# RWKV time mixing of a Perceiver block: token shift folded into the weights, keys kept in PSUM, gate moved into the denominator

## The chip, the cores and the metric

The kernel runs on one core of a Trainium2 chip, in float32. The metric is the device time of one execution in microseconds (us); lower is better. TensorE (PE) multiplies matrices into PSUM, VectorE (DVE), ScalarE (ACT) and GpSimd (POOL) work on tiles of 128 partitions, and loads and stores are issued from queues: SyncE (SP) carries most of them, ACT and POOL some.

## The reference

The program is a network of four layers; each has cross attention to a context, self attention or a relative of it, and a feed-forward part. X holds 8 sequences of 64 steps with 256 channels (512 tokens). The change lies in the second stage of layer 1, which mixes along time as RWKV does. For each sequence, with `xx` the input one step earlier (zero at the first):

```python
xk = x * time_mix_k + xx * (1.0 - time_mix_k)      # xv, xr alike
k = xk @ Wk.T; v = xv @ Wv.T; sr = sigmoid(xr @ Wr.T)
w = -exp(time_decay); u = time_first
def step(carry, kv):                                # along time, per channel
    aa, bb, pp = carry
    kt, vt = kv
    ww = u + kt
    p = max(pp, ww)
    e1 = exp(pp - p); e2 = exp(ww - p)
    y = (e1 * aa + e2 * vt) / (e1 * bb + e2)
    ww2 = pp + w
    p2 = max(ww2, kt)
    e1b = exp(ww2 - p2); e2b = exp(kt - p2)
    return (e1b * aa + e2b * vt, e1b * bb + e2b, p2), y
out = (sr * y) @ Wo.T
```

It is applied to a normalised X, and the result is added to X. `pp` keeps the exponents small: the sums aa and bb are stored relative to exp(pp).

## The kernel before

X stays in SBUF as 4 tiles (NI = 4) of 128 tokens by 256 channels. A stage normalises X (`normed`: statistics on DVE at L343 and L345, a power of -1/2 on POOL at L347, the scaling on DVE at L351), turns it with PE transposes (`transposed`, L378: tiles called pst) into `T`, two chunks (NC_ = 2) of 128 channels by 512 tokens, and multiplies it by weights: `lin_T` (L396, psl) gives a transposed result, `lin_nat` (L405, psn) a result in X's own layout. `into_X` (L1254) adds a PSUM tile into X. `evac` (L334 on ACT, L336 on DVE, in turns) copies a PSUM tile to SBUF.

The stages that matter, in order:

- f0, a mixture of experts. Its end: the experts' results are scattered to DRAM by indirect DMAs on POOL (L1234, 15 times in the last round), and `collect` loads them back in home order as `got` (L1249, tiles 0 and 2 from SP's queue, 1 and 3 from ACT's) and adds them to X (L1251). The experts' weights lie in a pool, `weights0`, that is closed after it.
- x1, the cross attention of layer 1: norm, projections (ends at L1622), then `flash` over the four tiles of tokens, which loads the context as `cn` and `ct` (L1630, L1632), takes maxima (L658), and exponentials (L671); its output goes into X at L1254.
- r1, the time mixing, L1671 to L1739. For k, v and r in turn DVE builds the mixed input: T times the share (L1689), plus T one step earlier times one minus the share (L1690; 504 of the 512 columns, since 8 first steps have no predecessor). PE multiplies by the weights, in 4 matmuls for each of the three. Keys kk and values vv are evacuated to SBUF, and r goes through Sigmoid on ACT (L1695). The recurrence runs along the 512 columns as DVE scans: pp (L1715) with a decay row whose value at each sequence's first step is -3e38, which resets it; then bb (L1728) and aa (L1729). The exponents e1, e2, f1, f2 each come from a difference on DVE and an Exp on ACT (L1716 to L1725). Then den = f1*bb + f2, the numerator f1*aa + f2*vv, a reciprocal (L1735), two products (L1736 and L1738, the second by the gate rr). All of that is done for each half c of the 256 channels.
- f1, another mixture of experts; it begins with X's norm and its transposes.

Weights are loaded by `weight(name)` (L307 to L313, the DMA at L312) into a rotating pool of six slots of 1 MB: x1q, x1kv, r1a (Wk and Wv), r1b (Wr and Wo), f1g, then the pairs f1up and f1dn of f1's experts. A slot's load waits until the last reader of what lay there is done. In f1, DVE, PE and the loads go on in step for eight experts.

A tile framework takes the instructions, gives each engine its own queue, and sets semaphores from the tiles that are read and written. The queue of an engine is in the order in which the framework schedules, by priority and readiness, not strictly in the order of the text[...]. Tiles with the same tag share space; pools that are closed give their space to later ones.

Of the kernel before, what the change touches and what calls it, by code (L numbers as in the profile page):

```python
# [11 lines left out]
F32 = mybir.dt.float32  # L12
AF = mybir.ActivationFunctionType
ALU = mybir.AluOpType
# [258 lines left out]
def perceiver(ctx: ExitStack, tc: tile.TileContext, d, col_at, row_at, const_at, out):  # L273
# [27 lines left out]
    def col(name, c=0):  # L301
        n, _ = col_at[name]
        return cols[:, n + c : n + c + 1]
# [3 lines left out]
    def weight(name, e=None):  # L307
        src = d[name] if e is None else d[name][e]
        n = src.shape[1]
        assert n <= WSLOT, (name, n)  # L310
        t = wpool.tile([P, WSLOT], F32, tag="w", name=f"w_{name}_{e}")
        nc.sync.dma_start(t[:, :n], src)  # L312
        return t[:, :n]  # L313

    def chunks(w, n):
        return w.rearrange("p (k n) -> p k n", n=n)
# [14 lines left out]
    def evac(dst, src):  # L331
        turn[0] ^= 1
        if turn[0]:
            nc.scalar.copy(dst, src)  # L334
        else:
            nc.vector.tensor_copy(dst, src)  # L336
# [916 lines left out]
    def into_X(i, t):  # L1253
        nc.vector.tensor_tensor(X[:, i, :], t, X[:, i, :], ALU.add)  # L1254
# [12 lines left out]
    def general(n=8):  # L1267
        return tc.tile_pool(name="ps", bufs=n, space=PSUM)
# [31 lines left out]
    with tc.tile_pool(name="l0res", bufs=1) as res, ExitStack() as both:  # L1300
# [38 lines left out]
        def fetch(b):  # L1339
            if b < B:  # L1340
                cns[b] = load_nat(cpool, b, 3)
# [261 lines left out]

    with tc.tile_pool(name="x1", bufs=1) as pool:
        wq = chunks(weight("x1q"), C)
        wkv = weight("x1kv")
# [15 lines left out]
        with ps as ps, psS as psS, psO as psO, fp as fp:  # L1624
# [36 lines left out]
                return dict(scores=scores, av=av, done=done, shift=qb[:, i : i + 1], before={1: [lambda: fetch(i + 1)] if i + 1 < NI else []})  # L1661

            fetch(0)
            flash(ps, psS, psO, fp, [tile_of(i) for i in range(NI)])
        with general() as ps:
            add_row_to_X("x1bv")
# [1 line left out]

    with general() as ps, tc.tile_pool(name="r1", bufs=1) as pool:  # L1671
        NC_ = C // P
        wkv, wro = chunks(weight("r1a"), C), chunks(weight("r1b"), C)
        xT = transposed(ps, normed(X))
        b4 = lambda x: x.rearrange("p c (b s) -> p c b s", s=S)
        g3 = lambda x: x.rearrange("p c (b s) -> p (c b) s", s=S)

        def big(name, n=NT):
            return pool.tile([P, NC_, n], F32, tag=name, name=name)

        om = pool.tile([P, 6], F32, tag="om", name="om")
        for n, k in enumerate("kvr"):
            for c in range(NC_):
                nc.vector.tensor_scalar(om[:, 2 * n + c : 2 * n + c + 1], col("time_mix_" + k, c), -1.0, 1.0, ALU.mult, ALU.add)
        kk, vv, rr = big("kk"), big("vv"), big("rr")
        for n, (k, w, dst) in enumerate((("k", wkv[:, 0:2], kk), ("v", wkv[:, 2:4], vv), ("r", wro[:, 0:2], rr))):
            mixed = pool.tile([P, NC_, NT], F32, tag="mixed", name="mixed", bufs=2)
            for c in range(NC_):
                nc.vector.tensor_scalar(mixed[:, c, :], xT[:, c, :], col("time_mix_" + k, c), None, ALU.mult)  # L1689
                nc.vector.scalar_tensor_tensor(  # L1690
                    b4(mixed)[:, c, :, 1:], b4(xT)[:, c, :, : S - 1], om[:, 2 * n + c : 2 * n + c + 1],
                    b4(mixed)[:, c, :, 1:], ALU.mult, ALU.add,
                )
            if k == "r":
                lin_T(ps, w, mixed, C, lambda c, t: nc.scalar.activation(rr[:, c, :], t, AF.Sigmoid))  # L1695
            else:
                lin_T(ps, w, mixed, C, lambda c, t: evac(dst[:, c, :], t))

        wd = pool.tile([P, NC_], F32, tag="wd", name="wd")
        n0, _ = col_at["time_decay"]
        nc.scalar.activation(wd, cols[:, n0 : n0 + NC_], AF.Exp)
        nc.vector.tensor_scalar(wd, wd, -1.0, None, ALU.mult)
        decay, pp, e1, e2, ev = big("decay"), big("pp"), big("e1"), big("e2"), big("ev")
        aa, bb, yy = big("aa"), big("bb"), big("yy")
        for c in range(NC_):
            nc.scalar.activation(decay[:, c, :], ones[:, 0:1].to_broadcast([P, NT]), AF.Copy, scale=wd[:, c : c + 1])
        nc.gpsimd.memset(g3(decay)[:, :, 0:1], -3.0e38)
        nc.gpsimd.memset(g3(e1)[:, :, 0:1], 0.0)  # L1710
        at = lambda x, c: b4(x)[:, c]
        old, new = (lambda x, c: at(x, c)[:, :, : S - 1]), (lambda x, c: at(x, c)[:, :, 1:])
        pmax, f1, f2, den = big("pmax"), big("f1"), big("f2"), big("den")
        for c in range(NC_):
            nc.vector.tensor_tensor_scan(pp[:, c, :], decay[:, c, :], kk[:, c, :], 0.0, ALU.add, ALU.max)  # L1715
            nc.vector.scalar_tensor_tensor(new(e1, c), old(pp, c), wd[:, c : c + 1], new(pp, c), ALU.add, ALU.subtract)  # L1716
            nc.scalar.activation(new(e1, c), new(e1, c), AF.Exp)
            nc.vector.tensor_tensor(e2[:, c, :], kk[:, c, :], pp[:, c, :], ALU.subtract)
            nc.scalar.activation(e2[:, c, :], e2[:, c, :], AF.Exp)
            u = col("time_first", c)  # L1720
            nc.vector.scalar_tensor_tensor(new(pmax, c), new(kk, c), u, old(pp, c), ALU.add, ALU.max)
            nc.vector.tensor_tensor(new(f1, c), old(pp, c), new(pmax, c), ALU.subtract)
            nc.scalar.activation(new(f1, c), new(f1, c), AF.Exp)
            nc.vector.scalar_tensor_tensor(new(f2, c), new(kk, c), u, new(pmax, c), ALU.add, ALU.subtract)
            nc.scalar.activation(new(f2, c), new(f2, c), AF.Exp)  # L1725
        for c in range(NC_):
            nc.vector.tensor_tensor(ev[:, c, :], e2[:, c, :], vv[:, c, :], ALU.mult)
            nc.vector.tensor_tensor_scan(bb[:, c, :], e1[:, c, :], e2[:, c, :], 0.0, ALU.mult, ALU.add)  # L1728
            nc.vector.tensor_tensor_scan(aa[:, c, :], e1[:, c, :], ev[:, c, :], 0.0, ALU.mult, ALU.add)  # L1729
            nc.vector.tensor_tensor(new(den, c), old(bb, c), new(f1, c), ALU.mult)  # L1730
            nc.vector.tensor_tensor(new(den, c), new(den, c), new(f2, c), ALU.add)
            nc.vector.tensor_tensor(new(f2, c), new(f2, c), new(vv, c), ALU.mult)
            nc.vector.tensor_tensor(new(f1, c), new(f1, c), old(aa, c), ALU.mult)
            nc.vector.tensor_tensor(new(f1, c), new(f1, c), new(f2, c), ALU.add)
            nc.vector.reciprocal(new(den, c), new(den, c))  # L1735
            nc.vector.tensor_tensor(new(f1, c), new(f1, c), new(den, c), ALU.mult)  # L1736
            nc.scalar.copy(at(f1, c)[:, :, 0:1], at(vv, c)[:, :, 0:1])
            nc.vector.tensor_tensor(yy[:, c, :], f1[:, c, :], rr[:, c, :], ALU.mult)  # L1738
        lin_nat(ps, wro[:, 2:4], yy, into_X)  # L1739

# [251 lines left out]
```

## Time and profile before

| | us |
|---|---|
| median of 3 runs | 2175.82 (2172.9 to 2176.54) |
| the profiled execution | 2174.78 |
| its span on the core | 2173.0 |
| mean granted clock of TensorE | 0.949 |
| first pst of x1's norm | 825.16 |
| first score matmul of x1 | 839.19 |
| first matmul of r1's projections | 895.95 |
| last product of r1 (yy) ends | 933.37 |
| last pst of f1's norm starts | 941.48 |

The last five rows are starts or ends in the span of the profiled execution. In the lines of the profile, "L396" is a line of the kernel, `out<-in` the tiles, and square brackets show for how long the engine was idle just before and who released it. A semaphore wait is put down to the one that came last. POOL's queue and SP's queue are as much queues as PE's.

### The profile page before, as it was taken

What the parts mean: (1) busy time and instruction counts of PE and PEld (TensorE: products, weight loads), DVE (VectorE), ACT (ScalarE), POOL (GpSimd) and SP (SyncE); (2) the same over time, 40 slices, a digit from 0 to 9 for tenths busy, and PEclk for the clock granted to TensorE, in tenths of its full rate; (3) what the DMA queues carried; (4) which work ended last, traced back from release to release, by engine and by line L of the source; (5) the groups of instructions that cost most, each with busy time, mean ns of one, the idle gap of its engine ahead of it and who ended that gap; (6) DMA issues with size and microseconds to landing.
All of it is one profiled execution on the core that took longest, in us unless ns stands there. A gap on an engine that the chain in (4) does not pass through costs nothing. (4 is left out here: it accounts for less than half of the span.)

```text
span 2173.0 us, 35537 instructions
## 1 busy us (share of the span) xinstructions
PE 1959.8 (90%) x14824; PEld 1398.1 (64%) x14824; DVE 1269.5 (58%) x2132; ACT 1025.3 (47%) x1672; POOL 310.8 (14%) x381
## 2 busy tenths in 40 slices
PE   5879999999987997569999999999899899998889
PEld 5546777777756574348567777778755566665747
DVE  6456777776627223750266666664623588888733
ACT  2326667666412222202255555552211788887323
POOL 3311111110033120030000000001000122222214
PEclk9989999999988998869999999999899999999979
DMA  6310000000014206116300001100111000000312
GB/s 232 116 47 1 17 17 16 17 17 11 11 61 170 95 34 260 70 42 236 129 16 32 32 32 42 37 1 30 59 49 60 30 33 17 17 18 16 132 61 100
DMA packets 33695, 130.97 MB, mean 60 GB/s; under 512 B 4408, under 2 KB 14272, under 8 KB 29056
## 3 DMA queue, kind: packets, MB, share of 16 engines
q1 hardware_dynamic: 29856, 120.57, 15.6%
q0 software_dynamic: 2592, 7.09, 0.9%
q8 instruction: 117, 1.92, 0.4%
q10 hardware_dynamic: 1088, 1.05, 0.1%
q14 instruction: 42, 0.34, 0.0%
HBM read 121.08 MB, written 13.66 MB: 62 GB/s over the span
## 5 line engine op out<-in xcount | busy, mean ns | idle before, releaser
L867 PEld LDWEIGHTS psav<-cn,raw 128*128 128x128 f32 (+1 forms) x3328 | 403.0, 192 | 88.5 <-issue 87.2
L802 DVE TENSOR_TENSOR raw<-raw,mb 128x1024 f32<-128x1024 f32 (+1 forms) x336 | 383.9, 1146 | 60.3 <-ACT mb L798 60.3
L867 PE MATMUL psav<-cn,raw 128*128 128x129 f32 (+1 forms) x3328 | 406.9, 275 | 0.7 <-ACT raw L806 0.7
L855 PE MATMUL psS<-qk,ct 128*128 128x512 f32 (+1 forms) x832 | 397.7, 600 | 6.8 <-ACT raw L856 6.8
L780 DVE TENSOR_TENSOR top<-raw,top 128x1024 f32<-128x1024 f32 (+1 forms) x240 | 271.4, 1131 | 152.6 <-ACT raw L856 123.4
L806 ACT ACTIVATE raw<-raw 128x1024 f32<-128x1024 f32 (+1 forms) x336 | 335.4, 1001 | 15.7 <-DVE raw L802 14.2
L856 ACT COPY raw<-psS 128x512 f32<-128x512 f32 (+1 forms) x416 | 236.3, 586 | 126.6 <-PE psS L855 123.4
L855 PEld LDWEIGHTS psS<-qk,ct 128*128 128x128 f32 (+1 forms) x832 | 140.7, 187 | 129.2 <-issue 95.5
L347 POOL TENSOR_TENSOR mv<-mv,mhalf 128x1 f32<-128x1 f32 x76 | 41.8, 553 | 872.1 <-DVE mv L346 861.4
L977 ACT COPY raw<-psS 128x1024 f32<-128x1024 f32 (+1 forms) x112 | 105.3, 940 | 2.2 <-PE psS L972 1.9
L774 DVE TENSOR_TENSOR top<-raw 128x1024 f32<-128x1024 f32 x48 | 58.8, 1226 | 70.9 <-ACT raw L856 36.8
L972 PEld LDWEIGHTS psS<-qz,kT 32*128 32x128 f32 (+1 forms) x1664 | 54.8, 181 | 61.5 <-ACT raw L977 33.7
L972 PE MATMUL psS<-qz,kT 32*128 32x128 f32 (+1 forms) x1664 | 77.0, 296 | 15.0 <-ACT raw L977 14.8
L993 PE MATMUL psav<-raw,v 128*32 128x128 f32 (+1 forms) x1664 | 87.2, 282 | 3.6 <-ACT raw L806 3.5
L993 PE MATMUL psav<-raw,ones 128*32 128x128 f32 (+1 forms) x1664 | 84.6, 275 | 0.0
L798 ACT COPY mb<-psmb 128x512 f32<-128x512 f32 x48 | 28.1, 585 | 96.9 <-PE psmb L796 96.8
L1208 PE MATMUL psgd<-w,xdT 128*128 x212 | 63.6, 436 | 0.8 <-DVE xdT L1197 0.4
L796 PE MATMUL psmb<-dg,ones 128*128 128x512 f32 x96 | 53.6, 640 | 7.9 <-POOL dg L790 4.6
L950 PE MATMUL psk<-ct,w_x3kv_None 128*128 128x401 f32 (+1 forms) x128 | 58.0, 539 | 0.7 <-ACT qT L334 0.7
L960 PE MATMUL psv<-w_x3kv_None,ct 128*128 128x256 f32 (+1 forms) x208 | 55.6, 388 | 0.0
L788 DVE TENSOR_REDUCE nm<-psm 128x4 f32<-128x512 f32 x48 | 33.0, 687 | 37.1 <-PE psm L786 36.8
L993 PEld LDWEIGHTS psav<-raw,v 128*32 128x32 f32 (+1 forms) x1664 | 41.1, 110 | 20.0 <-ACT raw L806 5.7
(438 smaller groups left out, 2948.4 us busy)
## 6 DMA issues: line engine op xcount, KB each, us to landing
cn<-in_cn_dram SPq DMA_DIRECT2D x24, 838.5 KB, 4.5
ct<-in_ct_dram SPq DMA_DIRECT2D x24, 800.5 KB, 4.5
w<-in_f0w_dram SPq DMA_DIRECT2D x8, 1088.0 KB, 15.5
w_f1up<-in_f1up_dram SPq DMA_DIRECT2D x8, 1024.0 KB, 4.9
w_f1dn<-in_f1dn_dram SPq DMA_DIRECT2D x8, 1024.0 KB, 4.8
w_f2w<-in_f2w_dram SPq DMA_DIRECT2D x8, 768.0 KB, 4.2
w<-in_f3w_dram SPq DMA_DIRECT2D x16, 384.0 KB, 7.6
dealt<-in_deal_dram SPq DMA_DIRECT2D x2, 2955.5 KB, 21.8
```

The costliest lines, as they stand in the source:

```text
L774: nc.vector.tensor_tensor(hd["top"], hd["raw", 0], raw, ALU.max)
L780: nc.vector.tensor_tensor(top[:n, :m, :], raw, top[:n, :m, :], ALU.max)
L802: nc.vector.tensor_tensor(raw, raw, halves[h]["mb"][:n].unsqueeze(1).to_broadcast([n, m, 512]), ALU.add)
L806: nc.scalar.activation(raw, raw, AF.Exp)
L855: nc.tensor.matmul(x[:n], ct[:, kt * P : kt * P + n], qk, start=True, stop=True)
L856: nc.scalar.copy(raw[:n, i, :], x[:n])
L867: nc.tensor.matmul(oa[:, j // 2, j % 2 * CO : (j % 2 + 1) * CO], w[:n, i, j * P : (j + 1) * P], cn[:n, kt, :], start=kt == 0 and j % 2 == ...
L950: nc.tensor.matmul(t[:, : hi - lo], wkv[:, c * P : (c + 1) * P], cts[b][:, lo:hi], start=True, stop=True)
L972: nc.tensor.matmul(x[:n, g, i * P : (i + 1) * P], kTs[h][r, kt * P : kt * P + n], qzs[b][r, c].rearrange("p m s -> p (m s)"), start=True, ...
L977: nc.scalar.copy(raw[:n, :m, :].rearrange("p i (g s) -> p i g s", g=4), x[:n, :, : m * P].rearrange("p g (i s) -> p i g s", s=P))
L993: nc.tensor.matmul(oa[r, at * P : (at + 1) * P], what, w[:n, i, g * P : (g + 1) * P], start=kt == 0 and at == 0, stop=kt == KT - 1 and at ...
L1208: nc.tensor.matmul(y[:, :m], st[t]["xT"][:, k, :], w[:, bass.ds(x + at + k * m, m)], start=k == 0, stop=k == C // P - 1)
```

## The change

Five things change in r1, and one new function is called within x1.

- The shares are multiplied into the weights instead of into the input: `mix_weights()` makes six pairs of 128x256 tiles, weight times share and weight times one minus share, on POOL, and it is called in x1 just before `flash`. It also makes wd (minus the exponential of the decay) and loads Wo into a tile of its own, `wo`. Its tiles are in the pool `mixw`, opened after `weights0` is closed.
- `mix(n)` then adds four matmuls on T and four on T one step earlier (504 columns) into one PSUM tile of two banks; there are three such tiles, for k, v and r. Keys are read from PSUM by the scan and by the differences. Values are copied by ACT.
- e1 and e2 come from one difference de: e1 = exp(-Relu(de)), e2 = exp(-Relu(-de)). f1 and f2 come from df in the same way. So there is no pmax, and there are two activations (Relu, Exp) for each.
- The gate: instead of y times sigmoid(r), den is multiplied by 1 + exp(-r) (`er`, with exp on ACT and a min and add on POOL), ahead of the reciprocal.
- ev, f2*vv and den*er are done on POOL.
- The output's eight matmuls write one PSUM tile, `mixed_out`, and the four additions follow.

In the order of the queues, POOL's om and first two products come ahead of the last scatter of f0, and the rest ahead of x1's four norm powers; SP's w_f1dn comes ahead of `got`; the loads of f1's weights move forward, since r1a and r1b are free earlier; ACT loads the table of exp ahead of `got`'s issue. The scheduler's order on ACT in r1 is e1, e2, f1, f2 of half 0, then e1 of half 1, the copies of vv, the rest of half 1, and er last.

```diff
--- before.py
+++ after.py
@@ -1603,6 +1603,28 @@
+    NC_ = C // P
+    mixing = ExitStack()
+    mixp = mixing.enter_context(tc.tile_pool(name="mixw", bufs=1))
+    mixw = mixp.tile([P, 3, 2, NC_, C], F32, tag="mixw", name="mixw")
+    wd = mixp.tile([P, NC_], F32, tag="wd", name="wd")
+    om = mixp.tile([P, 3, NC_], F32, tag="om", name="om")
+    wo = mixp.tile([P, NC_, C], F32, tag="wo", name="wo")
+    def mix_weights():
+        n0, _ = col_at["time_decay"]
+        nc.scalar.activation(wd, cols[:, n0 : n0 + NC_], AF.Exp)
+        nc.gpsimd.tensor_scalar(wd, wd, -1.0, None, ALU.mult)
+        nc.sync.dma_start(wo.rearrange("p k n -> p (k n)"), d["r1b"][:, 2 * C :])
+        r1a, r1b = chunks(weight("r1a"), C), chunks(weight("r1b"), C)
+        for n, (k, w) in enumerate((("k", r1a[:, 0:2]), ("v", r1a[:, 2:4]), ("r", r1b[:, 0:2]))):
+            for c in range(NC_):
+                share = col("time_mix_" + k, c)
+                nc.gpsimd.tensor_scalar(om[:, n, c : c + 1], share, -1.0, 1.0, ALU.mult, ALU.add)
+                nc.gpsimd.tensor_scalar(mixw[:, n, 0, c, :], w[:, c, :], share, None, ALU.mult)
+                nc.gpsimd.tensor_scalar(mixw[:, n, 1, c, :], w[:, c, :], om[:, n, c : c + 1], None, ALU.mult)
     with tc.tile_pool(name="x1", bufs=1) as pool:
         wq = chunks(weight("x1q"), C)
         wkv = weight("x1kv")
@@ -1661,6 +1683,7 @@
                 return dict(scores=scores, av=av, done=done, shift=qb[:, i : i + 1], before={1: [lambda: fetch(i + 1)] if i + 1 < NI else []})
             fetch(0)
+            mix_weights()
             flash(ps, psS, psO, fp, [tile_of(i) for i in range(NI)])
         with general() as ps:
             add_row_to_X("x1bv")
@@ -1668,75 +1691,84 @@
-    with general() as ps, tc.tile_pool(name="r1", bufs=1) as pool:
-        NC_ = C // P
-        wkv, wro = chunks(weight("r1a"), C), chunks(weight("r1b"), C)
+    with general(2) as ps, tc.tile_pool(name="r1", bufs=1) as pool, tc.tile_pool(name="r1p", bufs=1, space=PSUM) as held:
         xT = transposed(ps, normed(X))
         b4 = lambda x: x.rearrange("p c (b s) -> p c b s", s=S)
         g3 = lambda x: x.rearrange("p c (b s) -> p (c b) s", s=S)
-        def big(name, n=NT):
-            return pool.tile([P, NC_, n], F32, tag=name, name=name)
-        om = pool.tile([P, 6], F32, tag="om", name="om")
-        for n, k in enumerate("kvr"):
+        at = lambda x, c: b4(x)[:, c]
+        old, new = (lambda x, c: at(x, c)[:, :, : S - 1]), (lambda x, c: at(x, c)[:, :, 1:])
+        def big(name):
+            return pool.tile([P, NC_, NT], F32, tag=name, name=name)
+        def mix(n):
+            kvr = held.tile([P, NC_, NT], F32, tag=f"mix{n}", name="mix")
             for c in range(NC_):
-                nc.vector.tensor_scalar(om[:, 2 * n + c : 2 * n + c + 1], col("time_mix_" + k, c), -1.0, 1.0, ALU.mult, ALU.add)
-        kk, vv, rr = big("kk"), big("vv"), big("rr")
-        for n, (k, w, dst) in enumerate((("k", wkv[:, 0:2], kk), ("v", wkv[:, 2:4], vv), ("r", wro[:, 0:2], rr))):
-            mixed = pool.tile([P, NC_, NT], F32, tag="mixed", name="mixed", bufs=2)
-            for c in range(NC_):
-                nc.vector.tensor_scalar(mixed[:, c, :], xT[:, c, :], col("time_mix_" + k, c), None, ALU.mult)
-                nc.vector.scalar_tensor_tensor(
-                    b4(mixed)[:, c, :, 1:], b4(xT)[:, c, :, : S - 1], om[:, 2 * n + c : 2 * n + c + 1],
-                    b4(mixed)[:, c, :, 1:], ALU.mult, ALU.add,
-                )
-            if k == "r":
-                lin_T(ps, w, mixed, C, lambda c, t: nc.scalar.activation(rr[:, c, :], t, AF.Sigmoid))
-            else:
-                lin_T(ps, w, mixed, C, lambda c, t: evac(dst[:, c, :], t))
-        wd = pool.tile([P, NC_], F32, tag="wd", name="wd")
-        n0, _ = col_at["time_decay"]
-        nc.scalar.activation(wd, cols[:, n0 : n0 + NC_], AF.Exp)
-        nc.vector.tensor_scalar(wd, wd, -1.0, None, ALU.mult)
+                for k in range(NC_):
+                    nc.tensor.matmul(kvr[:, c, :], mixw[:, n, 0, k, c * P : (c + 1) * P], xT[:, k, :], start=k == 0, stop=False)
+                for k in range(NC_):
+                    nc.tensor.matmul(new(kvr, c), mixw[:, n, 1, k, c * P : (c + 1) * P], old(xT, k), start=False, stop=k == NC_ - 1)
+            return kvr
         decay, pp, e1, e2, ev = big("decay"), big("pp"), big("e1"), big("e2"), big("ev")
-        aa, bb, yy = big("aa"), big("bb"), big("yy")
+        f1, f2, de, df, er, vv = big("f1"), big("f2"), big("de"), big("df"), big("er"), big("vv")
+        aa, bb, den = big("aa"), big("bb"), big("den")
         for c in range(NC_):
             nc.scalar.activation(decay[:, c, :], ones[:, 0:1].to_broadcast([P, NT]), AF.Copy, scale=wd[:, c : c + 1])
         nc.gpsimd.memset(g3(decay)[:, :, 0:1], -3.0e38)
         nc.gpsimd.memset(g3(e1)[:, :, 0:1], 0.0)
-        at = lambda x, c: b4(x)[:, c]
-        old, new = (lambda x, c: at(x, c)[:, :, : S - 1]), (lambda x, c: at(x, c)[:, :, 1:])
-        pmax, f1, f2, den = big("pmax"), big("f1"), big("f2"), big("den")
+        nc.gpsimd.memset(g3(e2)[:, :, 0:1], 1.0)
+        nc.gpsimd.memset(g3(den)[:, :, 0:1], 1.0)
+        def weights(c, d, one, two):
+            for x, sign in ((one, 1.0), (two, -1.0)):
+                nc.scalar.activation(new(x, c), new(d, c), AF.Relu, scale=sign)
+                nc.scalar.activation(new(x, c), new(x, c), AF.Exp, scale=-1.0)
+        kk = mix(0)
+        pv = mix(1)
+        pr = mix(2)
         for c in range(NC_):
             nc.vector.tensor_tensor_scan(pp[:, c, :], decay[:, c, :], kk[:, c, :], 0.0, ALU.add, ALU.max)
-            nc.vector.scalar_tensor_tensor(new(e1, c), old(pp, c), wd[:, c : c + 1], new(pp, c), ALU.add, ALU.subtract)
-            nc.scalar.activation(new(e1, c), new(e1, c), AF.Exp)
-            nc.vector.tensor_tensor(e2[:, c, :], kk[:, c, :], pp[:, c, :], ALU.subtract)
-            nc.scalar.activation(e2[:, c, :], e2[:, c, :], AF.Exp)
-            u = col("time_first", c)
-            nc.vector.scalar_tensor_tensor(new(pmax, c), new(kk, c), u, old(pp, c), ALU.add, ALU.max)
-            nc.vector.tensor_tensor(new(f1, c), old(pp, c), new(pmax, c), ALU.subtract)
-            nc.scalar.activation(new(f1, c), new(f1, c), AF.Exp)
-            nc.vector.scalar_tensor_tensor(new(f2, c), new(kk, c), u, new(pmax, c), ALU.add, ALU.subtract)
-            nc.scalar.activation(new(f2, c), new(f2, c), AF.Exp)
+            nc.vector.scalar_tensor_tensor(new(de, c), new(kk, c), wd[:, c : c + 1], old(pp, c), ALU.subtract, ALU.subtract)
+            weights(c, de, e1, e2)
+            nc.scalar.copy(vv[:, c, :], pv[:, c, :])
+            nc.gpsimd.tensor_tensor(ev[:, c, :], e2[:, c, :], vv[:, c, :], ALU.mult)
+            nc.vector.scalar_tensor_tensor(new(df, c), new(kk, c), col("time_first", c), old(pp, c), ALU.add, ALU.subtract)
+            weights(c, df, f1, f2)
         for c in range(NC_):
-            nc.vector.tensor_tensor(ev[:, c, :], e2[:, c, :], vv[:, c, :], ALU.mult)
+            nc.scalar.activation(er[:, c, :], pr[:, c, :], AF.Exp, scale=-1.0)
+            nc.gpsimd.tensor_scalar(er[:, c, :], er[:, c, :], 1.0e36, 1.0, ALU.min, ALU.add)
+        for c in range(NC_):
             nc.vector.tensor_tensor_scan(bb[:, c, :], e1[:, c, :], e2[:, c, :], 0.0, ALU.mult, ALU.add)
-            nc.vector.tensor_tensor_scan(aa[:, c, :], e1[:, c, :], ev[:, c, :], 0.0, ALU.mult, ALU.add)
             nc.vector.tensor_tensor(new(den, c), old(bb, c), new(f1, c), ALU.mult)
             nc.vector.tensor_tensor(new(den, c), new(den, c), new(f2, c), ALU.add)
-            nc.vector.tensor_tensor(new(f2, c), new(f2, c), new(vv, c), ALU.mult)
+            nc.gpsimd.tensor_tensor(den[:, c, :], den[:, c, :], er[:, c, :], ALU.mult)
+            nc.gpsimd.tensor_tensor(new(f2, c), new(f2, c), new(vv, c), ALU.mult)
+            nc.vector.tensor_tensor_scan(aa[:, c, :], e1[:, c, :], ev[:, c, :], 0.0, ALU.mult, ALU.add)
+        for c in range(NC_):
             nc.vector.tensor_tensor(new(f1, c), new(f1, c), old(aa, c), ALU.mult)
             nc.vector.tensor_tensor(new(f1, c), new(f1, c), new(f2, c), ALU.add)
-            nc.vector.reciprocal(new(den, c), new(den, c))
-            nc.vector.tensor_tensor(new(f1, c), new(f1, c), new(den, c), ALU.mult)
             nc.scalar.copy(at(f1, c)[:, :, 0:1], at(vv, c)[:, :, 0:1])
-            nc.vector.tensor_tensor(yy[:, c, :], f1[:, c, :], rr[:, c, :], ALU.mult)
-        lin_nat(ps, wro[:, 2:4], yy, into_X)
+            nc.vector.reciprocal(den[:, c, :], den[:, c, :])
+            nc.vector.tensor_tensor(f1[:, c, :], f1[:, c, :], den[:, c, :], ALU.mult)
+        out_ = held.tile([P, NC_, NT], F32, tag="mix0", name="mixed_out")
+        t = out_.rearrange("p c n -> p (c n)")
+        for k in range(NC_):
+            for i in range(NI):
+                nc.tensor.matmul(
+                    t[:, i * C : (i + 1) * C], f1[:, k, i * P : (i + 1) * P], wo[:, k, :],
+                    start=k == 0 and i % 2 == 0, stop=k == NC_ - 1 and i % 2 == 1,
+                )
+        for i in range(NI):
+            into_X(i, t[:, i * C : (i + 1) * C])
+    mixing.close()
```

## Prediction

> **What bounds the kernel now.** I read the page first, then the stretch of the time mixing in the timeline, then the stretch ahead of it where the change puts its new work, and at last the groups of POOL by shape, because the change gives POOL work that this kernel never gave it here.
>
> The page's busy shares:
>
> ```profile
> span 2173.0 us, 35537 instructions
> PE 1959.8 (90%) x14824; PEld 1398.1 (64%) x14824; DVE 1269.5 (58%) x2132; ACT 1025.3 (47%) x1672; POOL 310.8 (14%) x381
> ```
>
> TensorE is busy for 90% of the whole, but that is an average over stages. The windows of the time mixing (span time; each pair is one engine's busy time and count, in the order PE, PEld, DVE, ACT, POOL) show another bound:
>
> ```profile
> 901.00:913.00 12.00, 7.19 (x17) 2.85 (x15) 11.90 (x19) 8.43 (x15) 0.00 (x0) 1.00 0.25 87
> 913.00:925.00 12.00, 0.00 (x0) 0.00 (x0) 12.00 (x14) 1.04 (x3) 0.00 (x0) 0.50 0.00 0
> ```
>
> From 901 to 925 VectorE never stops, and POOL does nothing. The timeline gives the edges:
>
> ```profile
> 895.95 8.80 PE L396 MATMUL psl<-mixed,w_r1a_None 128*128 128x512 f32 x16 [2.14 <-DVE mixed L1690]
> 901.29 1.23 DVE L1715 TENSOR_TENSOR_SCAN pp<-decay,kk 128x512 f32<-128x512 f32 x1
> 918.35 3.30 DVE L1735 RECIPROCAL den<-den 128x504 f32<-128x504 f32 x1
> 932.68 0.69 DVE L1738 TENSOR_TENSOR yy<-f,rr 128x512 f32<-128x512 f32 x1
> ```
>
> From the first scan to yy's end (933.4) are 32 us of VectorE; then come output matmuls, four additions and f1's norm, whose last transpose starts at 941.48: my mark for the end of the stage. So VectorE is what the change must relieve. The stretch ahead, from the experts' answers to x1's first attention scores:
>
> ```profile
> 812.32 0.96 POOL L1234 DMA_INDIRECT answered<-rows,homes  x1 [0.30 <-issue]
> 813.59 0.96 POOL L1234 DMA_INDIRECT answered<-rows,homes  x1 [0.30 <-ACT rows L1232]
> 816.14 0.89 SPq L1249 DMA_DIRECT2D got<-answered  x2
> 819.26 0.48 DVE L1251 SCALAR_TENSOR_TENSOR X<-got,pr,X 128x256 f32<-128x256 f32 x1 [8.30 <-DMA got<-answered]
> 824.02 1.71 POOL L347 TENSOR_TENSOR mv<-mv,mhalf 128x1 f32<-128x1 f32 x3 [9.47 <-DVE mv L345]
> 825.19 1.74 PE L378 MATMUL pst<-const,xn 128*128 128x128 f32 x6 [12.35 <-DVE mv L346]
> 842.63 1.28 ACT L671 ACT_TABLE_LOAD   x1 [4.91 <-DVE nm L661]
> ```
>
> This chain has no slack: last scatter, load of got, X additions, norm, transposes; PE idles 12.35 us in it. POOL looks free for 9.47 us, yet both of its ends (scatter, norm's power) are on the chain.
>
> **The change part by part: x1's start.** mix_weights() has twelve 128x256 products by a column, six tiny om operations and one on wd. By the order of the instructions on POOL, om and two products come ahead of the last scatter (their tile lies on the freed expert weights, which the last matmuls read), and all others ahead of x1's four norm powers. The prices, from POOL's groups by shape (busy us, mean ns):
>
> ```profile
> L1369 POOL TENSOR_SCALAR turned<-const,cols 128x128 f32<-128x128 f32 x4 | 2.4, 603 | 0.0
> L1371 POOL TENSOR_TENSOR shift<-shift,turned 128x128 f32<-128x128 f32 x4 | 1.7, 452 | 0.0
> L601 POOL TENSOR_TENSOR qkr<-qkr,shift 128x512 f32<-128x512 f32 x4 | 5.1, 1270 | 25.5 <-DVE qkr L598 25.5
> L1771 POOL TENSOR_SCALAR dw<-put,wt 128x128 f32<-128x128 f32 x32 | 12.5, 408 | 14.4 <-DVE put L1769 12.9 <-PE psget L1772 1.4
> L1002 POOL TENSOR_TENSOR res<-res,const 128x128 f32<-128x128 f32 x16 | 20.1, 1253 | 140.1 <-DVE res L1001 140.1
> ```
>
> Two shapes of one kind (0.452 for 128, 1.27 for 512) give 0.18 fixed. A product by a column takes 0.603 for 128, so 0.18 + 2 x 0.42 = 1.02 for 256; another form, L1771, would give 0.18 + 2 x 0.23 = 0.64. Between 0.64 and 1.2 I take 1.02: same form.
> - The last scatter: POOL is free at 813.3; om 0.2 (as the small copies, 0.196), 2 x 1.02 and a gap of 0.3 bring it to 815.9 instead of 813.59: +2.3 for everything that loads got.
> - Six more products of r1a follow, with om: the eighth ends about 816.8 + 6 x 1.02 + 0.9 = 823.9. On SP's queue the load of w_f1dn (1 MB) now stands before SP's two got loads, and its slot is r1a's: it waits for that eighth product. So got for tiles 0 and 2, issued at 816.14 before, is issued near 824.4, behind 1 MB that takes 4.8 us (the page's row for f1dn): tile 0 lands near 828.7, tile 2 by 829.5. Queued behind on SP are f1's next weights and x1's context, which still land before the scores. The two got loads on ACT's queue come with the scatter and are hidden.
> - The four additions still to come take 1.7; from the last addition to the first transpose were 2.3 (822.83 to 825.16). So the transposes start near 832.7 instead of 825.16: +7.5. VectorE has nothing else meanwhile; no cover is left.
> - The exp table is loaded for wd before got's issue and no longer at 842.63, where PE stands 2.89 us for L671: -1.3.
>
> x1: +6.2. Against the row stands a rule of the Trainium skill, "GPSIMD Engine Reference", section 4.1: one-input operations on GpSimd run roughly at line rate. VectorE's 128x512 by a column takes 0.48, so a product would cost about 0.25, the eighth be done at 817.7, and the same chain end 6.2 earlier: x1 would lose nothing. The row of 603 ns for 128 elements speaks for the trace; I follow it.
>
> **r1.** Removed: VectorE's mixing (L1689, L1690, six each, 0.44 and 0.65 apart), four evacuations of kk and vv half on ACT, pmax, ev, f2*vv, the product with rr; Sigmoid and two table loads of 1.28 on ACT. Added: twice the matmuls (48 records for the three projections against 24); 16 Relu and Exp instead of 8 Exp; on POOL ev, f2*vv, er and den*er, two each.
> - PE starts at 894.4, without the mixing, not 895.95. A projection is 8 matmuls, 16 records; 8.80 cold as in the row, 16 x 0.43 warm. Each consumer waits for its whole PSUM tile: mix(0) 903.2, mix(1) 910.1, mix(2) 917.0. The first scan is 1.9 later than 901.29.
> - ACT (0.52 to 0.61 each): e for half 0 by 907.5; vv by 911.7 and 912.8, e for half 1 912.2, f for half 1 914.9, er after mix(2) 917.6 and 918.2. The waits of VectorE for it are hidden behind what follows.
> - POOL in its order ev0 (911.7), f2*vv0, ev1 at 1.27: 915.7. aa1 on VectorE waits for ev1, and behind it in VectorE's queue stand den+ of half 1 and so f2*vv1, which starts at 919.4. Behind that on POOL are er0, er1 (two-operation form as L1771: 4 x 0.23 + 0.1 = 1.0 each; by the other row 1.85), then den0*er at 924.0.
> - The reciprocal waits for that: two of 3.30, then two products: end 932.0 (933.7 with er at 1.85).
> - L1002 ran 1.253 beside VectorE's two-input L802, against 0.452 alone; L601 was undisturbed. The same page, section 8, says that GpSimd shares SBUF ports with VectorE when that has two SBUF inputs. By the undisturbed row alone the end is 932.0; by the rule and L1002 three of these products run beside scans, +1.1 each: 935.3. I take 935.3, since aa and bb are such scans.
> - Output: all four additions wait for the last of eight matmuls. 8 records took 3.7 cold, so 16 take 5.2 to 6.9 from the first half's product; with four additions (0.39 apart) and 4.6 for the norm the last transpose is 11.6 behind: 946.9 instead of 941.48, +5.4 (range +1 to +9). VectorE's work falls from 32 to about 24 us, but the gap is filled by waits.
>
> Sum: 6.2 + 5.4 = +11.6. The profiled execution's own time is 2174.78 (span 2173.0, 1.78 around it): 2186.4. The median of the runs is 2175.82, 1.04 above: 2187.4.
>
> **The rivals.**
> 1. POOL is quick and undisturbed (products 0.64, no collisions): the eighth product is done at 820.8, 3.1 earlier, x1 +3.1; r1's products end at 932.0, +2.1. Sum +5.2: 2181. For it: L1771's 408 ns in the same instruction kind; against it: L1369 is the very form.
> 2. POOL is slower than taken (products 1.2, er 1.85, every product beside VectorE stretched): the eighth at 825.3, x1 +7.6; r1 +9. Sum +16.6: 2192.4. For it: 1253 ns in L1002.
> 3. The other side: VectorE's relief decides, because POOL runs at line rate. At 0.25 a product x1 loses nothing, and keeps part of the 1.3 if the eighth is done earlier still. In r1 with er at 0.4 and no collisions den0*er runs from 918.6 (ACT's second er at 918.2, then 0.4) to 919.9; two reciprocals of 3.3 end at 926.5, the last product at 927.9, the transpose 11.6 later at 939.5: -2.0. Sum -2.0 to -3.3, middle 2173.2. It decides from where r1 stays at that and a product costs under 0.5 (x1 is 8 x price - 2.0, by the two bullets on POOL and SP). Against it: no product by a column in this trace takes under 0.36 for 128 elements, half the size.
> 4. The change doesn't act: then the mixing would still be on VectorE. The order of instructions shows it is not, so this has no share.
>
> **How the numbers follow.** The predicted case has 0.55 (its own range 2183 to 2191), rival 1 has 0.26, rival 2 0.12, rival 3 0.07. This kernel's measurement can tell about 0.2% (4.35 us) from no change. Rival 1 lies across that bound, half below: 0.13 of it is no change, 0.13 slower. Rival 3 lies short of the bound on the other side; its unknowns are larger than the gap, so 0.04 of it goes beyond, 0.03 not. Slower: 0.55 + 0.12 + 0.13 = 0.80; within: 0.16; faster: 0.04. The range leaves out rival 3 and the outer ends of rivals 1 and 2: 2178 to 2194.
>
> **What would show it.** Right: the last L1234 near 815.9; SP's got after w_f1dn near 824; first pst of x1 near 832.7; POOL products near 1.0; no table load at flash; matmuls of r1 from 894.4 plus x1's delay, without a pause for 22.6 us; the reciprocal's wait ended by POOL den; from T copies to the last pst about 53 us, against 47.6. Wrong: products under 0.4, SP's got within 2 us of ACT's, or a reciprocal that follows VectorE's own work with no wait for POOL.

## The result, and the profile after

The changed kernel takes 2183.42 us in the median of five runs (2182.53 to 2187.34) against 2175.82 before; the ratio is 1.0044 with a 95% interval of 1.0029 to 1.0059, so it is slower by 6 to 13 us. The profiled execution took 2182.96, 8.2 above that of before, with a span of 2181.0.

The page's first lines after the change:

```profile
span 2181.0 us, 35592 instructions
PE 1962.7 (90%) x14848; PEld 1399.2 (64%) x14848; DVE 1257.7 (58%) x2099; ACT 1026.6 (47%) x1678; POOL 337.4 (15%) x410
```

VectorE has 12 us less to do, POOL 27 more, and the kernel is slower. The timeline (start and length in us, engine, line, operation) tells where. First x1's start, where POOL and SP's queue got new work ahead of old:

```profile
812.76 0.96 POOL L1234 DMA_INDIRECT answered<-rows,homes  x1 [0.31 <-issue]
...
813.93 0.94 POOL L1625 TENSOR_SCALAR mixw<-w_r1a_None,cols 128x256 f32<-128x256 f32 x1
...
815.95 1.03 POOL L1234 DMA_INDIRECT answered<-rows,homes  x1 [0.17 <-issue]
...
818.59 0.90 ACTq L1249 DMA_DIRECT2D got<-answered  x2
...
823.49 0.33 SPq L312 DMA_DIRECT2D w_f1dn<-in_f1dn_dram  x1
...
824.12 0.89 SPq L1249 DMA_DIRECT2D got<-answered  x2
...
829.02 0.48 DVE L1251 SCALAR_TENSOR_TENSOR X<-got,pr,X 128x256 f32<-128x256 f32 x1 [4.97 <-DMA got<-answered]
...
832.85 0.66 PE L378 MATMUL pst<-const,xn 128*128 128x128 f32 x2 [19.58 <-DVE mv L345]
```

The two products ahead of the last scatter move it to 815.95. SP's got comes 5.5 us after ACT's, because w_f1dn stands ahead of it in SP's queue and waits for the eighth product (done at 823.46): the queue keeps its order, though ACT's got, which needs the same scatter, was issued at 818.59. SP's got takes 5.0 us from issue to landing, where it took 3.7 before; the 1 MB of w_f1dn is under way at the same time. PE idles 19.58 us, 7.2 more than before, until the first transpose.

Then r1. Its first matmul starts at 899.39. In this and the later text, M is the start of the first such matmul (L1709 here) in the trace that is read.

```profile
908.41 1.22 DVE L1736 TENSOR_TENSOR_SCAN pp<-decay,mix 128x512 f32<-128x512 f32 x1 [9.17 <-PE mix L1711]
...
918.05 2.17 POOL L1752 TENSOR_TENSOR f<-f,vv 128x504 f32<-128x504 f32 x1
...
919.09 2.21 DVE L1753 TENSOR_TENSOR_SCAN aa<-e,ev 128x512 f32<-128x512 f32 x1
...
920.19 2.18 POOL L1740 TENSOR_TENSOR ev<-e,vv 128x512 f32<-128x512 f32 x1
...
922.40 1.22 DVE L1753 TENSOR_TENSOR_SCAN aa<-e,ev 128x512 f32<-128x512 f32 x1 [1.10 <-POOL ev L1740]
...
927.66 3.84 POOL L1746 TENSOR_SCALAR er<-er 128x512 f32<-128x512 f32 x2
...
931.47 2.47 POOL L1751 TENSOR_TENSOR den<-den,er 128x512 f32<-128x512 f32 x2
932.76 6.56 DVE L1758 RECIPROCAL den<-den 128x512 f32<-128x512 f32 x2 [3.95 <-POOL den L1751]
...
939.92 5.79 PE L1765 MATMUL mixed_out<-wo,f 128*128 128x256 f32 x16 [17.97 <-DVE f L1759]
```

Read the square brackets: VectorE, which before had the mixing to do here and then never stopped from 901 to 925, waits 9.17 for the doubled matmuls, then for POOL's ev, and 3.95 for POOL's den. The last product ends at 940.46 (M + 41.1), and its two halves come together, so that all 16 records of the output follow it, where half of them were hidden before. The windows (the same columns as before the change) show the hole in VectorE's work:

```profile
908.40:920.40 12.00, 12.00 (x29) 5.32 (x28) 10.80 (x11) 9.48 (x20) 3.59 (x3) 1.00 0.00 0
920.40:932.40 12.00, 1.55 (x4) 0.38 (x2) 6.17 (x8) 1.08 (x2) 8.31 (x5) 0.78 0.00 0
```

Where before two such stretches had VectorE at 11.90 and 12.00, the second now has it at 6.17, with POOL at 8.31.

To place the difference I set the same PE instruction of both traces side by side. Later in the changed kernel by:

| place | later by, us | added in the stage |
|---|---|---|
| ahead of the last scatters | 0.44 | (not the change) |
| first pst of x1 | 7.67 | +7.23 |
| x1's output, psn | 4.92 | -2.75 |
| last pst of f1's norm | 10.22 | +5.30 |
| end of the span | 8.0 | -2.2 |

So x1 lost 4.5 and r1 5.3, and 2.2 came back in stages that the change does not touch. Of r1's 5.3, the last product is 2.1: it ends 41.1 after M, where before it ended 39.0 after the first mixing operation (894.36). The stretch from there to the last pst is 3.1, 11.24 against 8.11, with the whole output exposed. The other 0.1 lies ahead of M.

Of the 2.2 that came back, 1.6 lie at the start of f2 (layer 2's mixture of experts), where TensorE's granted clock, the number behind the five engines, is at half for a shorter time. Before:

```profile
1558.12:1582.01 23.89, 16.89 (x45) 10.33 (x45) 8.51 (x31) 2.78 (x4) 2.90 (x2) 0.50 0.19 67
```

And after:

```profile
1568.78:1589.26 20.48, 13.46 (x40) 9.13 (x41) 8.37 (x31) 2.10 (x3) 2.89 (x2) 0.50 0.23 78
```

### The profile page after: what moved, and what is told of

It is laid out like the page before. It is cut to its first block, busy times and chain, and to the rows that moved or that the text cites. A ratio compares the mean times of both kernels' runs of the same rounds, so it can differ in the third digit from the quotient of the medians.

```text
span 2181.0 us, 35592 instructions
## 1 busy us (share of the span) xinstructions
PE 1962.7 (90%) x14848; PEld 1399.2 (64%) x14848; DVE 1257.7 (58%) x2099; ACT 1026.6 (47%) x1678; POOL 337.4 (15%) x410
## 5 line engine op out<-in xcount | busy, mean ns | idle before, releaser
L1353 POOL TENSOR_SCALAR cmv<-cmv 128x13 f32<-128x13 f32 x8 | 8.0, 997 | 317.5 <-ACT raw L806 287.8
L378 PE MATMUL pst<-const,xn 128*128 128x128 f32 x64 | 17.2, 393 | 42.2 <-DVE mv L345 21.9
```

## The experiments

The totals are ratios to the kernel before, run on the same chip. "From the scatters" means: counted from the last scatter but one (L1234), which in these traces lies up to 2.5 us from its place before, for reasons ahead of the change. One profile locates a wait to some hundredths, while runs of one kernel differ by several us; for the stages I therefore go by the traces.

**1. The products later.** The changed kernel, its shares read through copies that depend on x1's qb.

```diff
-                share = col("time_mix_" + k, c)
+                share = late[:, n, c : c + 1]
+                nc.vector.scalar_tensor_tensor(share, q[:, 0:1], 0.0, col("time_mix_" + k, c), ALU.mult, ALU.add)
...
-            mix_weights()
+            mix_weights(qb)
```

> The changed kernel, but the twelve products on POOL read their shares through a copy that needs x1's qb, so they come after x1's norm, while flash runs; r1 is that of the changed kernel. Theory (the products hold up the last scatter, SP's load of got behind w_f1dn, and so x1's norm): SP's got is issued within 1 us of ACT's, the first pst of x1 is back near 825.5 (832.85 in the changed kernel), the gain at the exponentials of flash stays (x1's psn near 883.5 against 885.96 before), and from there to f1's last pst it takes as long as in the changed kernel (60.8 us from psn to the last pst, against 55.5 before). Total near 2176 to 2178, some 7 under the changed kernel. Rival (POOL's products take SBUF ports from VectorE wherever they lie): products of 1.2 us and more beside flash's VectorE operations, psn not before 886, total over 2180.

Measured: 2175.76, ratio 1.0002 (0.9994 to 1.0011), where the changed kernel has 1.0044 and, run again, 1.0039: some 8 to 9 us less. The timeline:

```profile
814.21 0.96 POOL L1234 DMA_INDIRECT answered<-rows,homes  x1 [0.30 <-ACT rows L1232]
...
817.20 0.89 SPq L1249 DMA_DIRECT2D got<-answered  x2
...
826.21 1.74 PE L378 MATMUL pst<-const,xn 128*128 128x128 f32 x6 [12.76 <-DVE mv L346]
...
840.34 0.93 POOL L1627 TENSOR_SCALAR mixw<-w_r1a_None,late 128x256 f32<-128x256 f32 x1
...
883.97 1.99 PE L405 MATMUL psn<-w_x1kv_None,oT 128*128 128x256 f32 x8 [0.35 <-ACT oT L1681]
```

The products run at 0.91 to 0.93 beside flash and hurt nothing there: from the scatters, x1's output (psn) is 2.6 earlier than before. From psn to f1's last pst (944.94) it takes 61.0, as in the changed kernel. The rival falls: it is their place that cost. That the total equals that of before is partly luck: from the scatters, f1's last pst is still 2.8 later than before, and 2.3 of that come back in later stages, as in the changed kernel.

**2. The two halves of x1's delay.** The kernel before, with the products made at the changed kernel's place and read by nothing (r1 reads the weights themselves):

> The kernel before, with the twelve products made on POOL at the place where the changed kernel makes them, and read by nothing; r1 still reads the weights themselves, so w_f1dn cannot come early and SP's two loads of got have nothing ahead of them. Theory (two delays: the products ahead of the last scatter, 2.3, and SP's queue, the larger part of the 7.7): first pst of x1 2.3 to 3.6 later than 825.16 (the norm's powers stand behind the last product on POOL, near 827.3), no table gain, r1 as before: total 2.3 to 3.6 over before. Rival (the products on POOL alone are the whole delay): 7 or more over before.

Measured: 2178.5, ratio 1.002 (1.0011 to 1.0029). From the scatters (0.9 earlier in this trace), the first pst is 3.2 later than before, and so is every later point up to f1. The norm's first power starts the moment the last product is done (from the timeline):

```profile
825.45 0.91 POOL L1677 TENSOR_SCALAR mixw<-w_r1b_None,om 128x256 f32<-128x256 f32 x1
...
826.34 1.71 POOL L347 TENSOR_TENSOR mv<-mv,mhalf 128x1 f32<-128x1 f32 x3
```

So POOL's queue alone costs 3.2; by subtraction the other 4.0 of the 7.2 belong to SP's queue. The direct test takes got off that queue and leaves POOL's as it is:

```diff
-            (nc.scalar if i % 2 else nc.sync).dma_start(g, home[:, i])
+            (nc.scalar if i % 2 or acts else nc.sync).dma_start(g, home[:, i])
...
-        collect(pool, (r, e2))
+        collect(pool, (r, e2), True)
```

> The changed kernel, but all four loads of got in f0's collect are issued from ACT's queue, so none stands behind w_f1dn on SP's; POOL's queue is unchanged. Theory (of the 7.2 us by which x1's norm is later, about 4 come from SP's queue and about 3 from POOL's): the first pst of x1 starts near 828.9 instead of 832.85, set by the norm's powers behind the last product on POOL; from then on as the changed kernel, f1's last pst near 947.7 (951.70), total 4 lower. Rival (POOL's products, or the loads themselves beside 1 MB of f1dn, set the norm's start whatever the queue): 831.5 or later, total within 1 of the changed kernel.

Measured: the first pst at 828.89, as expected; but the total did not follow, 2185.15, ratio 1.0048 (1.0032 to 1.0065). Against the changed kernel, and from the scatters, the first pst is 3.6 earlier; of that 2.35 is left at x1's first psn, 1.6 at M (897.46) and 0.4 at f1's last pst (950.92). Two things are seen on the way. The norm's other powers and flash's second scores come late (their matmuls take 2.72 where the changed kernel has 1.72, with the DMA engines busy at 413 GB/s in those four us). And at r1's start TensorE's clock is at half from 889.14 to 902.79, where the changed kernel has it at half from 896.35 to 903.18: the earlier start meets a full clock no sooner. So SP's queue is shown to hold the first pst by 3.6; that its removal alone is worth 4 us in time is refuted.

**3. The table load.** The kernel before, with the exponential of the decay ahead of flash and no longer in r1:

```diff
             fetch(0)
+            n0, _ = col_at["time_decay"]
+            nc.scalar.activation(wd, cols[:, n0 : n0 + NC_], AF.Exp)
+            nc.gpsimd.tensor_scalar(wd, wd, -1.0, None, ALU.mult)
             flash(ps, psS, psO, fp, [tile_of(i) for i in range(NI)])
```

> The kernel before, only with the exponential of the decay (and minus it, on POOL) made just ahead of flash, so that the table of exp is loaded ahead of got's issue and not at flash's first exponential. Theory (the load costs its 1.28, and because PE then idles 2.89 us in front of the second tile of scores, the granted clock falls to half for one step of 3.4 us, which costs about 1.5 more): PE's idle time there is 1.6, the clock of x1's scores stays at 1.00, and x1's psn comes 2.8 earlier than 885.96; r1 as before; total 2.8 lower than before. Rival (the load alone): 1.3 lower.

Measured in the trace: from the scatters, the transposes behind the scores come 2.7 earlier. The second tile of scores, in the kernel before:

```profile
844.98 3.26 PE L1639 MATMUL psS<-ct,qk 128*64 128x512 f32 x8 [2.89 <-ACT P L671]
```

In this kernel:

```profile
844.26 1.73 PE L1644 MATMUL psS<-ct,qk 128*64 128x512 f32 x8 [1.61 <-ACT P L671]
```

PE waits 1.28 less, which is the load, and the eight matmuls take 1.53 less. That second part is the clock: the windows over four us show it, in the number behind the five engines. The kernel before:

```profile
843.00:847.00 4.00, 2.02 (x6) 0.77 (x8) 0.64 (x3) 2.84 (x4) 0.00 (x0) 0.72 0.93 354
```

This kernel:

```profile
843.00:847.00 4.00, 2.74 (x17) 1.41 (x19) 2.16 (x4) 2.43 (x4) 0.00 (x0) 1.00 0.82 290
```

But in time it is worth nothing: 2175.02, ratio 1.0001 (0.9992 to 1.001). The trace shows it given back in two places. At f1's last pst 2.4 of it is left. Then both kernels run f1's start at half clock, and in both the clock comes back at the same time, 971.02 before and 971.43 here, though this kernel is ahead; 1.2 is left. The half-clock stretch before:

```profile
940.30:971.02 30.72, 21.43 (x71) 14.07 (x70) 14.46 (x59) 2.57 (x5) 15.42 (x34) 0.50 0.14 51
```

And of this kernel:

```profile
930.47:971.43 40.96, 29.11 (x88) 18.52 (x89) 20.22 (x80) 2.58 (x5) 17.15 (x37) 0.50 0.17 55
```

The rest goes at layer 2's first projection, where the clock of before is full:

```profile
1056.00:1062.00 6.00, 4.33 (x11) 2.02 (x12) 1.79 (x3) 0.68 (x2) 2.77 (x2) 1.00 0.97 397
```

And this kernel's is at half for 3.4 us:

```profile
1056.76:1060.18 3.42, 2.83 (x4) 1.28 (x5) 0.53 (x1) 0.51 (x1) 1.78 (x1) 0.50 1.02 421
```

The lengths of these stretches have a pattern. In the clock records of all twelve traces the granted clock is either full or half, and every stretch between two changes is a whole number of steps of 3.41 us: 30.72 is 9 of them, 40.96 is 12. So a gain of 2 or 3 us need not come out as it went in: it can be spent at half clock until the same change, or meet one step more or less later on. Why a step falls where it does, these runs don't show.

**4. POOL's part of r1.** The changed kernel with all of r1's POOL products on VectorE (four times `nc.gpsimd` to `nc.vector` in the loops of r1), and with er alone moved:

> The changed kernel with r1's ev, f2*vv, er's min and add, and den*er on VectorE instead of POOL; x1's start is unchanged. Theory (the POOL chain, er at 1.92 each above all, sets the start of the reciprocals): though VectorE gets eight operations, about 4.5 us, more, its waits of 1.1, 1.1 and 3.95 us go, the first reciprocal starts near 928 (932.76), the last product ends near 936 (940.46), f1's last pst near 947.3 (951.70): total 4 under the changed kernel. Rival (VectorE is the bound of r1 again as soon as it gets this work): the last product ends at 940 or later, total within 1 of the changed kernel or above.

> The changed kernel with only er's min and add moved from POOL to VectorE; ev, f2*vv and den*er stay on POOL. M is the start of the first L1709 matmul of r1; in the changed kernel the last product of r1 ends at M + 41.1, with everything of r1's POOL work on VectorE at M + 37.2. Theory (er, 1.92 each on POOL, is what the reciprocals wait for): den*er follows f2*vv of half 1 at once, the first reciprocal starts 3.5 to 3.9 earlier, last product at M + 37.4, total 3.5 to 4 under the changed kernel. Rival (the collisions of ev and f2*vv with the scans set the pace as much): less than 2.5 gained, M + 39 or later.

Measured, all moved: the first reciprocal at M + 28.8, the last product at M + 37.2 (M + 41.1), f1's last pst at M + 45.5 (M + 52.3). VectorE does more and is done 3.8 earlier, where 4.5 was expected; the tail is 3 shorter than expected, since the order now finishes one half first and its output matmuls are hidden again. Total: 2175.31, ratio 1.0012 (1.0 to 1.0024), about 7 under the changed kernel. Eight of its twelve runs took 2173.8 to 2176.7 and four 2182.9 to 2185.6, and the trace is of one of the four (2183.26): in it, 3.0 of the 6.0 gained at f1's last pst go at layer 2's first projection, with two steps at half clock from 1064.25 to 1071.07, where the kernel before has it full. So the stage's gain is shown, and its worth in time is not one number. er alone: last product at M + 38.5, so er is 2.5 of the 3.8, and the rest lies in the other three products; that is between theory and rival. Its timeline shows ev and f2*vv as slow as before, and den*er behind er:

```profile
917.40 2.17 POOL L1752 TENSOR_TENSOR f<-f,vv 128x504 f32<-128x504 f32 x1
...
927.67 0.76 DVE L1746 TENSOR_SCALAR er<-er 128x512 f32<-128x512 f32 x2
928.24 2.53 POOL L1751 TENSOR_TENSOR den<-den,er 128x512 f32<-128x512 f32 x2 [1.20 <-DVE er L1746]
```

In time er alone gave nothing that can be told: ratio 1.0041 (1.0026 to 1.0056).

**5. The whole-tile wait.** The changed kernel with a PSUM tile for each half of k, v and r, and two for the output:

```diff
-            kvr = held.tile([P, NC_, NT], F32, tag=f"mix{n}", name="mix")
-            for c in range(NC_):
+            t = held.tile([P, NT], F32, tag=f"mix{n}{c}", name="mix")
```

> The changed kernel with a PSUM tile of one bank for each half of k, v and r (and two for the output, of two token tiles each), instead of one tile of two banks for both halves: a reader waits for its own half. All else is unchanged. Theory (the wait for the whole tile costs): the first scan starts at M + 5.6 instead of M + 9.0, the exponentials follow, and the last product ends 2 to 3 earlier than M + 41.1, with f1's last pst following within 11: total 2 to 3 under the changed kernel. Rival (POOL's chain behind er hides it, since er waits for r, the last projection): the scan is earlier, the last product stays within 1 of M + 41.1.

Measured: first scan at M + 5.6, last product at M + 36.3, 4.8 earlier, twice the forecast; f1's last pst at M + 44.4; ratio 1.0026 (1.0018 to 1.0033). It is not a clean undoing of one wait: the output's tile is split as well, and since er of half 0 now comes earlier, the scheduler also puts den*er of half 0 ahead of er of half 1 on POOL, so the two reciprocals are apart and half of the output is hidden. What of the 4.8 is the wait and what the order, these runs don't separate.

**6. The moves together.** The products late and r1's POOL work on VectorE:

> Both moves of the first experiments at once: the products on POOL behind x1's qb, and r1's ev, f2*vv, er and den*er on VectorE. Theory (both losses are separate): x1's psn 2.2 earlier than before, r1 from M to f1's last pst 45.5 (52.3 in the changed kernel, 47.1 from the same point before): f1's last pst near 938 against 941.48 before, total 3 to 4 under before. Rival (a gain of a few us is given back where TensorE's clock comes back a step later, as with the early table alone): total within 1.5 of before.

Measured: 2168.69, ratio 0.9975 (0.9965 to 0.9985): 5 us faster than before, more than forecast. At f1's last pst it is 4.8 ahead of before, from the scatters; another 2.7 come in later stages, so part of the surplus is luck. Then the halves apart, values read from PSUM, and the gate in one operation, which leaves out the min on er:

```diff
-            nc.gpsimd.tensor_scalar(er[:, c, :], er[:, c, :], 1.0e36, 1.0, ALU.min, ALU.add)
-            nc.gpsimd.tensor_tensor(den[:, c, :], den[:, c, :], er[:, c, :], ALU.mult)
+            nc.vector.scalar_tensor_tensor(den[:, c, :], er[:, c, :], 1.0, den[:, c, :], ALU.add, ALU.mult)
```

> The moves of b1, and in r1: a PSUM tile for each half of k, v and r, each half's products, reciprocal and output matmuls as early as that half allows, values read from PSUM by VectorE without a copy, no min on er (exp(-r) is used as it is), and (er + 1)*den in one VectorE operation; four PSUM tiles for the output. Theory (r1 was lengthened by waits on whole tiles and POOL, while its VectorE work is shorter): first scan at M + 5.6, last product at M + 33.5, f1's last pst at M + 40.2, near 933 against 941.48 before: total 7 to 9 under before, so about 2166 to 2169. Rival (VectorE or the doubled matmuls bound it): last product at M + 37 or later, total no better than b1.

Measured: 2168.19, ratio 0.9971 (0.996 to 0.9982), faster than both kernels, but no faster than the version just shown. The stage did what was forecast: last product at M + 32.4, f1's last pst at M + 40.5 (933.72). The timeline:

```profile
898.82 1.22 DVE L1738 TENSOR_TENSOR_SCAN pp<-decay,mix 128x512 f32<-128x512 f32 x1 [5.78 <-PE mix L1713]
...
913.55 3.34 DVE L1756 RECIPROCAL den<-den 128x512 f32<-128x512 f32 x1
...
921.45 3.34 DVE L1756 RECIPROCAL den<-den 128x512 f32<-128x512 f32 x1
```

From the scatters, it leads the kernel before by 9.7 at f1's start, the version before it by 4.8; at the end of the span both lead by some 7. Its window at layer 2's first projections shows the clock at 0.63:

```profile
1049.00:1055.00 6.00, 4.19 (x8) 1.80 (x8) 1.13 (x3) 0.58 (x1) 2.90 (x2) 0.63 0.97 388
```

That of the version before it, at the same work, shows 1.00:

```profile
1054.00:1060.00 6.00, 4.40 (x11) 2.02 (x12) 1.80 (x3) 0.76 (x2) 2.70 (x2) 1.00 0.98 400
```

**7. The changed kernel again.**

> The changed kernel once more on this chip, beside the kernel before. Theory (the stages differ by the same amounts in every execution; only the steps of TensorE's clock in other stages vary): from the last round of scatters to f1's last pst again 9.8 us longer than before, total 6 to 12 over before. Rival (the first profile's stage times were an accident): the sum up to f1's last pst differs by more than 1 us from 9.8.

Measured: 2182.32, ratio 1.0039 (1.0025 to 1.0053). From the scatters to f1's last pst it is 9.75 longer than before, against 9.78 in the first profile: the stage times repeat.

## Why the prediction was right

The forecast was 2187.4 with slower at 0.80; measured were 2183.4, slower, inside the range. The mechanism is the one forecast: POOL and SP's queue hold x1's start, and waits fill the time that VectorE saves in r1. Of the 4.0 too much, 1.7 lie in x1, 0.1 in r1 and 2.2 in stages that the sum left out. Step by step:

- **x1's start** was forecast +7.5 and is +7.23. The last scatter was forecast at 815.9 and came at 815.95; the eighth product at 823.9, and it ended at 823.46. Of these times 0.44 is not the change (the table's first row), so both came some 0.4 to 0.9 sooner than forecast, and the slower landing of got (4.9 from its issue to the first addition, where 4.3 was taken) made up for most of it. The products take 0.92 to 0.94 alone and 1.15 to 1.17 beside the additions to X, where 1.02 was taken. The rule of the Trainium skill that one-input operations run roughly at line rate on GpSimd ("GPSIMD Engine Reference", section 4.1) would have put x1's loss at nothing; 0.92 for 256 elements, against 0.48 for 512 on VectorE, decides for the row. Experiments 1 and 2 show both causes, POOL's queue and SP's.
- **The table load** is the term that was mis-sized: -1.3 forecast, -2.75 measured. The forecast counted the load's 1.28 alone; with PE's idle time a step at half clock went too, worth 1.5, which experiment 3 shows.
- **r1** was forecast +5.4 and is +5.30, but two terms within it were off and cancelled by luck. er costs 1.92 on POOL, not 1.0; the product-by-column row, which gave 1.85, was the nearer one. The collisions cost about 1.8 of the end, not 3.3, by subtraction: with er at 1.85 the forecast without them was M + 39.3, measured M + 41.1. Where they hit, a product of 1.27 became 2.17 beside scans, and the scans were hit as well (1.22 becoming 2.21). Not every overlap did so: ev of half 0 kept its 1.27, though the scan of bb ran beside its last 0.85 and took 1.94.
- The whole-tile waits came out within 0.2 (the first scan at M + 9.0, forecast M + 8.8; er, which needs the third projection, at M + 22.6 as forecast), and the tail was 11.24 against 11.6.
- **What the sum left out**: 2.2 us given back in layers 2 and 3. The forecast had no term for stages that the change doesn't touch. Only the trace of the unchanged later stages shows it. At f2's start the changed kernel has a half-clock stretch of six steps where before it has seven, and that is most of the 2.2. What decides which of the two a kernel gets is open.
- Of the rivals, quick POOL is out by the products' 0.92 and by er; slow POOL is right for er, but not for the products by a column. VectorE's relief became real in experiments 4, 5 and 6: from M to f1's last pst 45.5, 44.4, and 45.3 and 40.5 us, where before it took 47.1 from the first mixing operation. In experiment 5 POOL is still in the chain (the first reciprocal waits 2.17 for den), so POOL's work alone was not what held it back: splitting the tiles, with the order that came with it, gained as much.

## What to carry to other kernels

An engine that stands idle in a stretch may still hold both ends of the chain there. Before giving it work, read what comes next in its queue and in the queues of the loads whose slots that work keeps: here twelve products of 0.92 us held the first transpose by 7 us at their place, and by 0.4 when they ran 26 us later. And taking work off the engine that bounds a stage pays only if what it then reads is ready when it asks: here a whole PSUM tile of two halves, and the results of a slower engine, were not.

## What the runs showed of the hardware

- A stall of PE costs more than its length when the granted clock follows: a table load of 1.28 us cost 2.7 in its stage, the clock being 0.72 over four us instead of 1.00, with one step of 3.4 us at half.
- A gain of 2 to 3 us in one stage is not a gain in time. With the early table the stage was 2.7 shorter and the total the same; 9.7 at f1's start became about 7 at the end. The granted clock changed only between half and full, and only in whole steps of 3.41 us, so such a gain can be lost, or grow, at the next change.
- Where POOL and VectorE ran together, both could be slowed: a scan with two SBUF inputs took 2.21 instead of 1.22 beside f2*vv and ev, which took 2.17 and 2.18 instead of 1.27.
